# Projecting q and k of fourteen batches with seven quarter products instead of eight, on one Trainium2 core

## The chip, the cores and the metric

The kernel runs on one core of one Trainium2 chip. The metric is the device time of one launch in microseconds (us). All arithmetic is fp32.

## The reference, cut to what matters

`x` is 16 batches of 256 tokens by 512 features. First comes an attention layer with a residual, then a GRU over the 256 steps with a residual.

```
xn  = rms_norm(x) * g_norm * (1 + scale) + shift      # scale, shift from cond @ W_emb + b_emb
qkv = xn @ W_qkv                                      # 512 x 1536: q, k, v, 16 heads of 32
q, k = rms_norm(q) * g_q, rms_norm(k) * g_k           # per head of 32
o   = softmax(q k^T / sqrt(32)) v ;  x = x + o + o @ W_out
x   = x + GRU(x, W_ih, W_hh, b_ih, b_hh, h0 = cond)   # 256 steps, 16 batches side by side
```

The change is in one product of this: the 256 x 512 `xn` of a batch with the 512 x 1024 columns of `W_qkv` that give q and k.

## The kernel before, in words

The program has a short start (projection of `cond`, batch 0), then the attention of the 16 batches, then the GRU. The order of TensorE, VectorE, ScalarE and GpSimd is written out by hand: each engine runs its instructions in the order in which the code records them, and an instruction that waits holds up all that stand behind it on its engine. SyncE's DMA issues are ordered by a scheduler.

Attention is a pipeline over slots. Batch `b` has four slots, one for each group `g` of four heads. In slot `g` of batch `b` TensorE first makes the logits of the group (`logits_by_key`, L606, into the four PSUM banks `lg0` to `lg3`). ScalarE takes their exponentials (`exps_by_key`, L620) and GpSimd adds the two halves of each (`sums`, L622). The group of the slot before is multiplied with v (`weigh_by_key`, L634 and L644) and VectorE divides it (`put_weighed_by_key`, L658 to L663: transpose, reciprocal, transpose, multiply). Between these stand the steps for batch `m = b+1`: its q and k are projected (`project_qk`, L281, four calls of 64 matrix instructions), squared on ScalarE (L294), summed by head on VectorE (L298), turned to a factor (`Rsqrt`: L183, then Ln and Exp on ScalarE, L185 and L186, then three small VectorE operations, L190 to L193), multiplied by it (`norm_qk`, L309), transposed (`turn_qk`, L324), and q is scaled on GpSimd (`scale_q`, L334); v is projected (`project`, L262) and copied out by ScalarE (`put_v`, L303). Steps for batch `b+2` turn its tokens (`turn_x`, L236, `put_x`, L252 and L254), and steps for batch `b+3` take its token norms (`norm_first`, L209) and apply them (`norm_apply`, L220).

Every matrix product of this stage is cut into four column groups of 32 outputs that run side by side (the index `j`), and each fp32 product takes two matrix instructions. A call of `project_qk` makes 64 tokens by 1024 columns, with 256 moving columns in an instruction:

```
for k in ks:
    for i in range(2):
        t = n * P + 64 * m + 32 * i
        for j in range(HG):
            nc.tensor.matmul(a[32 * j : 32 * j + 32, i * T : (i + 1) * T],
                             batches[b].xnT[:, k, t : t + 32], w[:, k, j], ...)
```

The remaining four PSUM banks, `A`, `X`, `Y` and `Z`, hold the projections, the turned tokens and the weighed groups in turn. `w_a` is one 24 KB region in a partition: `W_emb` at the start, the normed tokens `xs` and the `squares` during attention, and `W_ih` for the GRU; `w_b` (`wq`) holds `W_qkv` and later `W_hh`.

Of the kernel before, what the change touches and what calls it, by code (L numbers as in the profile page):

```python
# [8 lines left out]
F32 = mybir.dt.float32  # L9
AF = mybir.ActivationFunctionType  # L10
ALU = mybir.AluOpType
# [9 lines left out]
def kernel(  # L21
# [69 lines left out]
    def load_tokens(xt, b):  # L91
        nc.sync.dma_start(xt, x[b].rearrange("(n p) d -> p n d", p=P))
# [26 lines left out]
    def program(ctx, bounded):  # L119
# [4 lines left out]
        small = work.enter_context(tc.tile_pool(name="small", bufs=4))  # L124
        ps_lg = ctx.enter_context(tc.tile_pool(name="ps_lg", bufs=1, space=PSUM))
        ps = ctx.enter_context(tc.tile_pool(name="ps", bufs=1, space=PSUM))
        x_tiles = dict(enumerate(x_first))

        def load_x(b):
            xt = p2.tile([P, NT, D], F32, tag="x", name=f"x_{b}")  # L130
            load_tokens(xt, b)
            x_tiles[b] = xt

        xs = w_a[:, KC * 2 * D : KC * 2 * D + NT * D].rearrange("p (n d) -> p n d", n=NT)
        squares = w_a[:, KC * 2 * D + NT * D : KC * 3 * D].rearrange("p (i n) -> p i n", i=2)
        wih = w_a.rearrange("p (k n) -> p k n", k=KC)

        b_more = p1.tile([P, 2, P], F32, name="b_more")

# [28 lines left out]
        def tile_ps(name, bank, shape=(P, D)):  # L168
            pool = ps if len(bank) == 1 else ps_lg
            return pool.tile(list(shape), F32, tag=bank, name=name)  # L170
# [31 lines left out]
        def norm_first(b, parts=range(NT)):  # L202
            if parts[0] == 0:
                batches[b].ssx = small.tile([P, NT], F32, tag="ssx", name=f"ssx_{b}")
                batches[b].rs = Rsqrt(batches[b].ssx, D, NT, f"x{b}")
            for n in parts:

                unused = xs[:, n, :] if b != 2 else spare(f"squares_{n}")
                nc.scalar.activation(  # L209
                    unused, x_tiles[b][:, n, :], AF.Square,  # L210
                    accum_out=batches[b].ssx[:, n : n + 1],
                )

# [4 lines left out]
        def norm_apply(b, rstd):  # L218
            for n in range(NT):
                nc.vector.tensor_scalar(  # L220
                    xs[:, n, :], x_tiles[b][:, n, :], rstd[:, n : n + 1],
                    None, ALU.mult,
                )
            batches[b].xnT = p1.tile([P, KC, T], F32, tag="xnT", name=f"xnT_{b}", bufs=2)
            if 0 < b and b + 2 < B:
                load_x(b + 2)

# [8 lines left out]
                nc.tensor.transpose(dst[r], src[q], ident[q, q])  # L236

        def turn_x(b, banks):
            tps = [tile_ps(f"tpx_{b}_{r}", banks[r], (P, KC, NT, QR)) for r in range(R)]
            for c in range(KC):  # L240
                for n in range(NT):
                    turn_block(
                        [tp[:, c, n, :] for tp in tps], xs[:, n, c * P : (c + 1) * P]
                    )
            return tps
# [25 lines left out]
        def project_qk(b, n, m, ks, a):  # L271
# [17 lines left out]
                        )  # L289
            return a  # L290

        def square(b, n, s, a):
            sq = spare(f"sq_{b}_{n}_{s}") if b == 0 else squares[:, s]
            nc.scalar.activation(sq, a, AF.Square)  # L294
            return sq
# [4 lines left out]
        def put_v(b, n, a):  # L300
            if n == 0:
                batches[b].v = p2.tile([P, NT, D], F32, tag="v", name=f"v_{b}")
            nc.scalar.copy(batches[b].v[:, n, :], a)  # L303

        def norm_qk(b, n, accs, rstd):
            out = []
            for s in range(2):
                qk = p1.tile([P, H, DH], F32, tag="qkn", name=f"qkn_{b}_{n}_{s}", bufs=2)
                nc.vector.tensor_tensor(  # L309
                    qk,  # L310
                    accs[s].rearrange("p (h d) -> p h d", d=DH),
                    rstd[:, s * H : (s + 1) * H].unsqueeze(2).to_broadcast([P, H, DH]),
                    ALU.mult,
                )
                out.append(qk.rearrange("p h d -> p (h d)"))
            return out
# [345 lines left out]
            nc.vector.transpose(rden, inv.to_broadcast([P, T // DH, DH]))  # L662
            nc.vector.tensor_tensor(oT[:, w.g, :, w.b], w.o[:, 0, :], rden, ALU.mult)  # L663

        def fast_slot0(b, w, prev, st):
            m = b + 1
            if b == 0:
                project(b, 1, 2, (3,), st.v1)
            put_v(b, 1, st.v1)
            exps_by_key(w)  # L670
            if b == 0:
                put_x(1, 0, st.tpx)
                put_x(1, 1, st.tpx, engine=nc.scalar)
                batches[2].rs.first()
                norm_apply(2, batches[2].rs.second())
            weigh_by_key(prev, "Y")
            st.q = project_qk(m, 0, 0, range(KC), "A")
            put_weighed_by_key(prev)
            tpx = turn_x(b + 2, "ZY") if b + 2 < B else None
            st.s0 = Stats(m, 0)  # L680
            sq = st.s0.square(0, st.q)
            if tpx:
                put_x(b + 2, 0, tpx)
                put_x(b + 2, 1, tpx, engine=nc.scalar)
            st.k = project_qk(m, 0, 1, (0, 1, 2), "X")
            st.s0.add(0, sq)

        def fast_slot1(b, w, prev, st):
            m = b + 1
            exps_by_key(w)  # L690
            project_qk(m, 0, 1, (3,), st.k)
            weigh_by_key(prev, "Y")
            put_weighed_by_key(prev)
            sq = st.s0.square(1, st.k)
            st.q1 = project_qk(m, 1, 0, range(KC), "Z")
            st.s0.add(1, sq)
            st.s0.rs.first()
            if b + 3 < B:
                norm_first(b + 3, (0,))
            st.s1 = Stats(m, 1)  # L700
            st.rstd = st.s0.rs.second()
            st.sq = st.s1.square(0, st.q1)

        def fast_slot2(b, w, prev, st):
            m = b + 1
            exps_by_key(w)
            qk0 = norm_qk(m, 0, (st.q, st.k), st.rstd)
            k = project_qk(m, 1, 1, (0, 1), "Y")
            weigh_by_key(prev, "X")
            project_qk(m, 1, 1, (2, 3), k)  # L710
            turn_qk(m, 0, qk0)
            scale_q(m, 0)
            put_weighed_by_key(prev)
            sq = st.s1.square(1, k)
            st.s1.add(0, st.sq)
            st.v0 = project(m, 0, 2, (0, 1), "A")
            st.s1.add(1, sq)
            st.s1.rs.first()
            if b + 3 < B:
                norm_first(b + 3, (1,))  # L720
                batches[b + 3].rs.first()
            if b == 0:
                for c in range(KC):
                    d = wo[:, c, c * P : (c + 1) * P]
                    nc.vector.tensor_tensor(d, d, ident, ALU.add)
                load_small()
            elif b == 2:
                for i in range(2):
                    a = b_rows[:, 2 * i, :]
                    nc.vector.tensor_tensor(a, a, b_more[:, i, :], ALU.add)  # L730
            st.accs = (st.q1, k)

        def fast_slot3(b, w, prev, st):
            m = b + 1
            exps_by_key(w)
            if b == 4:
                load_rows(wih, w_ih, (0, 1))
            elif b == 6:
                for i in range(4):
                    load_block(i)  # L740
            elif b == B - 3:
                load_rows(wih, w_ih, (2,))
            elif m == B - 1:
                load_rows(whh, w_hh, cols=slice(0, 2 * D))
                load_rows(wih, w_ih, (3,))
            qk1 = norm_qk(m, 1, st.accs, st.s1.rs.second())
            project(m, 0, 2, (2, 3), st.v0)
            st.v1 = project(m, 1, 2, (0, 1), "X")
            weigh_by_key(prev, "Z")
            project(m, 1, 2, (2, 3), st.v1)  # L750
            turn_qk(m, 1, qk1)
            scale_q(m, 1)
            put_v(m, 0, st.v0)
            put_weighed_by_key(prev)
            if b + 3 < B:
                norm_apply(b + 3, batches[b + 3].rs.second())
            if m == B - 1:
                put_v(m, 1, st.v1)

        TI = 16  # L760
        first = []
# [163 lines left out]
        with tc.manual_schedule(engines=ORDERED):  # L925
# [48 lines left out]
            for ks, n in (((0,), 0), ((0,), 1), ((1,), 0), ((1,), 1), ((2, 3), 0), ((2, 3), 1)):  # L974
                for i in range(2):
                    accs[n][i] = project_qk(0, n, i, ks, accs[n][i])
            v = project(0, 0, 2, range(KC), "lg0")
            s0, s1 = Stats(0, 0), Stats(0, 1)
            norm_first(1)
            batches[1].rs.first()  # L980
# [23 lines left out]
            for b in range(B - 1):  # L1004
                for g in range(NG):
                    if bounded:
                        w = logits_by_key(b, g)
                        (fast_slot0, fast_slot1, fast_slot2, fast_slot3)[g](b, w, prev, st)
                    else:
                        w = logits(b, g)  # L1010
                        (slot0, slot1, slot2, slot3)[g](b, w, prev, st)
                    prev = w
# [233 lines left out]
```

## Time and profile before

| | |
|---|---|
| median of 3 runs | 1658.77 us (1658.73 to 1660.42) |
| the profiled execution: its own time, its span | 1657.48 us, 1655.7 us |
| busy: TensorE, VectorE, ScalarE, GpSimd | 1638.1, 909.5, 536.7, 271.3 us |
| attention, slots of batches 0 to 14 | 34.4 to 508.2 us |
| one batch of it, from the same slot to the same slot | 31.5 us |
| busy in such a batch: VectorE, ScalarE, GpSimd | 18.2, 15.7, 12.6 us |
| granted TensorE clock | 0.999 |

The profile shows one execution, its times counted from the start of the span. 1.8 us of the execution's own time lie outside the span, and the execution was 1.3 us faster than the median of the runs. In a row of the timeline stand start, length, engine, source line and operation, the tiles written and read with their shapes, and the number of instructions merged in the row; in brackets stands the idle time before it and what ended it. The length of a row of matrix instructions runs to the modelled end of its last one, and the next row begins before that: rates are read from start to start. `PE` is TensorE, `DVE` VectorE, `ACT` ScalarE, `POOL` GpSimd.

### The profile page before, as it was taken

How to read it: one execution, taken by the hardware profiler on the slowest of the kernel's cores; microseconds unless marked ns; L12 is line 12 of the kernel's file. 1: busy time of each engine (PE TensorE's matmuls, PEld its weight loads, DVE VectorE, ACT ScalarE, POOL GpSimd, SP SyncE). 2: the span in 40 equal slices, each digit the busy share in tenths (PEclk: the TensorE clock that was granted, in tenths of full speed). 3: DMA queues.
4: the chain of work that ended last, by engine and by line, in shares of the span. 5: the costliest groups of instructions: out<-in, count | busy, mean ns of one | idle time of the engine just before them, and what ended most of it. 6: DMA issues, size and time to landing. Idle time of an engine off the chain costs nothing.

```text
span 1655.7 us, 93929 instructions
## 1 busy us (share of the span) xinstructions
PE 1638.1 (99%) x42901; PEld 1254.2 (76%) x42901; DVE 909.5 (55%) x3060; ACT 536.7 (32%) x1728; POOL 271.3 (16%) x534
## 2 busy tenths in 40 slices
PE   8999999999999999999999999999999999999997
PEld 4554554554555888888888888888888888888886
DVE  4566565556555555555555555555555555555554
ACT  4455444454443222222222222222222222222222
POOL 0334343343341000000000000000000000000000
PEclk9999999999999999999999999999999999999999
DMA  5300000000004000100000000000000010000000
GB/s 215 92 15 16 26 15 15 28 15 15 14 14 105 25 17 17 23 23 17 17 17 22 22 20 17 17 19 22 23 17 17 17 24 17 11 11 11 14 14 18
DMA packets 51178, 44.35 MB, mean 27 GB/s; under 512 B 10407, under 2 KB 43475, under 8 KB 50771
## 3 DMA queue, kind: packets, MB, share of 16 engines
q1 hardware_dynamic: 50663, 38.20, 8.6%
q8 instruction: 337, 5.52, 1.4%
q14 instruction: 70, 0.57, 0.1%
q10 hardware_dynamic: 108, 0.06, 0.0%
HBM read 29.79 MB, written 8.39 MB: 23 GB/s over the span
## 4 chain that ended last, share of the span: by engine, by line
PE 96%; DVE 2%; ACT 1%; issue 1%; DMA 0%; ACTq 0%; DVEq 0%
PE gr L807 26%; PE gz L807 19%; PE gn L807 14%; PE qk L281 14%; PE qkv L262 7%; PE o L1035 6%; PE lg L606 4%; PE o L634 3%; PE o L644 2%; PE tpx L236 1%; PE first L768 0%; DVE trh L1084 0%; ACT n L1163 0%; DVE n L1161 0%; DVE n L1162 0%
## 5 line engine op out<-in xcount | busy, mean ns | idle before, releaser
L807 PE MATMUL gr<-w_a,xT 128*32 128x256 f32 x4096 | 267.7, 379 | 0.0
L281 PE MATMUL qk<-w_b,xnT 128*32 128x256 f32 x4096 | 238.6, 380 | 1.2 <-DVE xnT L254 1.2
L1157 ACT ACTIVATE r<-trr 128x64 f32<-128x64 f32 x256 | 65.5, 256 | 514.8 <-DVE trr L1084 512.8
L1084 DVE STREAM_TRANSPOSE trr<-gr 128x128 f32<-128x128 f32 x256 | 81.1, 317 | 274.8 <-PE gr L807 274.8
L622 POOL TENSOR_TENSOR sums<-e 128x256 f32<-128x256 f32 x240 | 168.3, 733 | 310.0 <-ACT e L620 310.0
L281 PEld LDWEIGHTS qk<-w_b,xnT 128*32 128x32 f32 x4096 | 128.8, 110 | 92.5 <-issue 9.5
L807 PEld LDWEIGHTS gr<-w_a,xT 128*32 128x32 f32 x4096 | 133.1, 110 | 84.6
L1163 ACT ACTIVATE n<-n 128x64 f32<-128x64 f32 x256 | 65.6, 256 | 308.1 <-DVE n L1162 305.2
L620 ACT ACTIVATE e<-lg 128x512 f32<-128x512 f32 x256 | 131.9, 602 | 54.1 <-PE lg L606 54.0
L1035 PE MATMUL o<-oT,wo 128*32 128x256 f32 x1920 | 147.3, 379 | 0.0
L1084 DVE STREAM_TRANSPOSE trh<-gn 128x128 f32<-128x128 f32 x256 | 81.0, 317 | 116.9 <-PE gn L807 116.9
L807 PE MATMUL gr<-w_b,padded 128*32 128x128 f32 x4096 | 135.7, 273 | 2.7 <-DVE padded L1191 1.4
L807 PEld LDWEIGHTS gr<-w_b,padded 128*32 128x32 f32 x4096 | 114.7, 110 | 30.5 <-DVE padded L1191 29.9
L807 PE MATMUL gz<-w_b,padded 128*32 128x128 f32 x4096 | 135.3, 273 | 0.0
L807 PE MATMUL gn<-w_b,padded 128*32 128x128 f32 x4096 | 135.3, 273 | 0.0
L807 PE MATMUL gz<-w_a,xT 128*32 128x128 f32 x4096 | 135.3, 273 | 0.0
L807 PE MATMUL gr<-w_b,h 128*16 128x128 f32 x4064 | 134.3, 273 | 0.4
L807 PE MATMUL gz<-w_b,h 128*16 128x128 f32 x4064 | 134.2, 273 | 0.0
L807 PE MATMUL gn<-w_b,h 128*16 128x128 f32 x4064 | 134.2, 273 | 0.0
L807 PEld LDWEIGHTS gz<-w_a,xT 128*32 128x32 f32 x4096 | 117.2, 110 | 21.9
L1193 POOL TENSOR_TENSOR y<-xT,padded 128x64 f32<-128x64 f32 x128 | 41.0, 320 | 534.9 <-DVE padded L1191 534.9
L1193 POOL TENSOR_TENSOR y<-xT,h 128x64 f32<-128x64 f32 x127 | 40.7, 321 | 499.1 <-DVE h L1191 499.1
(125 smaller groups left out, 2233.4 us busy)
## 6 DMA issues: line engine op xcount, KB each, us to landing
xin<-in_x_dram SPq DMA_DIRECT2D x256, 32.0 KB, 2.5
out_dram<-osb SPq DMA_DIRECT2D x248, 32.0 KB, 2.5
x<-in_x_dram SPq DMA_DIRECT2D x14, 512.0 KB, 3.4
w_b<-in_L_cond_W_qkv_dram SPq DMA_DIRECT2D x4, 768.0 KB
w_a<-in_L_cond_W_ih_dram SPq DMA_DIRECT2D x16, 192.0 KB, 4.8
w_a<-in_L_cond_W_emb_dram SPq DMA_DIRECT2D x4, 512.0 KB, 3.5
w_b<-in_L_cond_W_hh_dram SPq DMA_DIRECT2D x16, 128.0 KB, 3.2
oT<-in_x_dram SPq DMA_DIRECT2D x2, 512.0 KB
```

The lines of the kernel that those rows point to most:

```text
L262: nc.tensor.matmul(a[32 * j : 32 * j + 32, :], batches[b].xnT[:, k, n * P + 32 * j : n * P + 32 * j + 32], wq[:, k, s * D : (s + 1) * D], ...
L281: nc.tensor.matmul(a[32 * j : 32 * j + 32, i * T : (i + 1) * T], batches[b].xnT[:, k, t : t + 32], w[:, k, j],  start=(k == 0 and i == 0), ...
L606: nc.tensor.matmul(w.lg[i][:, k, :], batches[b].qkT[r, NG + g, k * P : (k + 1) * P], batches[b].qkT[r, g, :], start=True, stop=True,)
L620: nc.scalar.activation(w.e[i], w.lg[i], AF.Exp)
L622: nc.gpsimd.tensor_tensor(w.sums[:, i, :], w.e[i][:, 0, :], w.e[i][:, 1, :], ALU.add)
L634: nc.tensor.matmul(w.o[i * DH : (i + 1) * DH, 0, :], v[:, k, h * DH : (h + 1) * DH], w.e[i][:, k, :], start=(k == 0), stop=(k == NT - 1),)
L807: nc.tensor.matmul(dst[32 * j : 32 * j + rows], stationary, w[:, k, :].rearrange("p (g j c) -> p j g c", g=3, c=P)[:, j, first::2][:, : ds ...
L1035: nc.tensor.matmul(acc[32 * j : 32 * j + 32, :], w[:, k, P * j + 32 * m : P * j + 32 * m + 32], rhs, start=(k == 0), stop=(k == KC - 1),)
L1084: nc.vector.transpose(tr.rearrange("p q s b -> p (q s b)"), gate)
L1157: nc.scalar.activation(r, turned("r", t, gr[:, 0, :])[:, :, s, :], AF.Sigmoid)
L1163: nc.scalar.activation(n, n, AF.Tanh)
L1193: (nc.gpsimd if t + 1 < T else nc.vector).tensor_tensor(y[:, :, tl * B : (tl + 1) * B], xTs[grp][:, :, ti, :], h, ALU.add)
```

## The change

The product of a batch is cut in two along the tokens (`n`), the contraction (`i`) and the columns (`h`: heads 0 to 7 and 8 to 15 of both q and k). Eight quarter products of 128 x 256 by 256 x 512 would give the four results. The change makes them from seven, by Strassen's scheme in the form with three sums of weights plus one made in place (`T3`, `T2`, `T4`, and `W01 - W00` in the place of `W01`), made once, and four sums of x (`S1` to `S4`) for each batch. All these sums run on GpSimd.

- Batches 0 and 1 are projected as before. From batch 2 on (`b >= 1`), the slots are `quarter_slot0` to `quarter_slot3`; the old functions serve `b = 0` alone as `first_slot0` to `first_slot3`.
- `multiply` makes one quarter product: 64 matrix instructions of 128 moving columns.
- The products stay in PSUM and are added up there where they can be: `z` in bank `A` takes four products in turn, `q7` in bank `Y` two, `q2` in bank `X` one. Three states of `z` are copied to SBUF by ScalarE (`keep`), and VectorE adds them to the others (`add_kept`).
- `norm_quarters` norms and transposes two results at a time and has GpSimd scale their q half. Three of the four results are normed from SBUF and not from PSUM.
- The order of the slots is new. A batch begins in slot 3 of the batch before (`begin_quarters`). Projection of v stands in slots 1, 2, 3 and the next slot 0. The turned tokens go to `lg2` and `lg3` and not to `Z` and `Y`.
- Weight sums lie in the first half of `w_a`, x sums in the next sixth. So `W_ih` is loaded only in slot 3 of batch 14, with the first four blocks of GRU input and two thirds of `W_hh`. Token tiles come from the pool of the GRU's input blocks, by two DMAs a batch and not one.

```diff
...
+        def add_weights(dst, a, op, b):
+            for k in range(2):
+                nc.gpsimd.tensor_tensor(dst[:, k], a[:, k], b[:, k], op)
+        def make_w_sums():
+            add_weights(w_sum(T3), w_half(1, 1), ALU.subtract, w_half(0, 1))
+            add_weights(w_sum(T2), w_sum(T3), ALU.add, w_half(0, 0))
+            add_weights(w_sum(T4), w_half(1, 0), ALU.subtract, w_sum(T2))
+        def make_last_w_sum():
+            add_weights(w_half(0, 1), w_half(0, 1), ALU.subtract, w_half(0, 0))
...
+        def make_x_sum(b, i):
+            a, op, c = {
+                S1: (x_part(b, 1, 0), ALU.add, x_part(b, 1, 1)),
+                S2: (x_sums[:, S1], ALU.subtract, x_part(b, 0, 0)),
+                S3: (x_part(b, 0, 0), ALU.subtract, x_part(b, 1, 0)),
+                S4: (x_part(b, 0, 1), ALU.subtract, x_sums[:, S2]),
+            }[i]
+            nc.gpsimd.tensor_tensor(x_sums[:, i], a, c, op)
+        def multiply(a, stationary, w, name=None):
+            start = isinstance(a, str)
+            if start:
+                a = tile_ps(name, a)
+            w = w.rearrange("p k s (g j d) -> p k j s g d", j=HG, d=DH)
+            for k in range(2):
+                for i in range(4):
+                    for j in range(HG):
+                        nc.tensor.matmul(
+                            a[32 * j : 32 * j + 32, i * P : (i + 1) * P],
+                            stationary[:, k, 32 * i : 32 * i + 32],
+                            w[:, k, j],
+                            start=(start and k == 0 and i == 0),
+                            stop=(k == 1),
+                            skip_group_check=True,
+                        )
+            return a
...
+        def norm_quarters(b, which, accs, rstd, fresh):
+            for s in range(2):
+                n, h = which[s]
+                a = dst = accs[s].rearrange("p (h d) -> p h d", d=DH)
+                if fresh[s]:
+                    dst = p1.tile([P, D], F32, tag="qkn", name=f"c_{b}_{n}_{h}", bufs=3)
+                    dst = dst.rearrange("p (h d) -> p h d", d=DH)
+                nc.vector.tensor_tensor(
+                    dst, a,
+                    rstd[:, s * H : (s + 1) * H].unsqueeze(2).to_broadcast([P, H, DH]),
+                    ALU.mult,
+                )
+                t = slice(n * P, (n + 1) * P)
+                nc.vector.transpose(
+                    batches[b].qkT.rearrange("p (s h g) t -> p s h g t", s=2, h=2)[
+                        :, :, h, :, t
+                    ].rearrange("p s g (i t) -> p i s g t", i=4),
+                    dst.rearrange("p h d -> p (h d)"),
+                )
+                q = batches[b].qkT[:, 2 * h : 2 * h + 2, t]
+                nc.gpsimd.tensor_scalar(q, q, g_col, 1.0, ALU.mult, ALU.mult)
...
+        def begin_quarters(m, st):
+            st.z = multiply("A", x_part(m, 0, 0), w_half(0, 0), f"z_{m}")
+            st.q7 = multiply("Y", x_sums[:, S3], w_sum(T3), f"q7_{m}")
+            st.z1 = keep(m, 1, st.z)
+        def quarter_slot0(b, w, prev, st):
+            m = b + 1
+            if b == 1:
+                put_v(b, 1, st.v1)
+            exps_by_key(w)
+            weigh_by_key(prev, "X")
+            if b > 1:
+                project(b, 1, 2, (2, 3), st.v1)
+                put_v(b, 1, st.v1)
+            tpx = turn_x(b + 2, ("lg2", "lg3")) if b + 2 < B else None
+            put_weighed_by_key(prev)
+            if tpx:
+                put_x(b + 2, 0, tpx)
+                put_x(b + 2, 1, tpx, engine=nc.scalar)
+            a = multiply("X", x_part(m, 0, 1), w_half(1, 0), f"q2_{m}")
+            st.c11 = add_kept(m, 0, 0, a, st.z1)
+            multiply(st.z, x_sums[:, S2], w_sum(T2))
+            st.z2 = keep(m, 2, st.z)
+        def quarter_slot1(b, w, prev, st):
+            m = b + 1
+            exps_by_key(w)
+            multiply(st.z, x_sums[:, S1], w_half(0, 1))
+            weigh_by_key(prev, "X")
+            z4 = keep(m, 4, st.z)
+            st.sa, st.sb = Stats(m, 0), Stats(m, 1)
+            sq = st.sa.square(0, st.c11)
+            st.c22 = add_kept(m, 1, 1, st.q7, z4)
+            st.sa.add(0, sq)
+            put_weighed_by_key(prev)
+            multiply(st.z, x_sums[:, S4], w_half(1, 1))
+            sq = st.sa.square(1, st.c22)
+            st.v0 = project(m, 0, 2, (0,), "Z")
+            if m + 1 < B:
+                make_x_sum(m + 1, S3)
+            st.sa.add(1, sq)
+            st.sa.rs.first()
+            sq = st.sb.square(0, st.z)
+            st.ra = st.sa.rs.second()
+            st.sb.add(0, sq)
+            if b + 3 < B:
+                norm_first(b + 3, (0,))
+        def quarter_slot2(b, w, prev, st):
+            m = b + 1
+            batches[m].qkT = p1.tile([P, 2 * NG, T], F32, tag="qkT", name=f"qkT_{m}", bufs=2)
+            exps_by_key(w)
+            norm_quarters(m, ((0, 0), (1, 1)), (st.c11, st.c22), st.ra, (False, False))
+            weigh_by_key(prev, "X")
+            multiply(st.q7, x_part(m, 1, 1), w_sum(T4))
+            put_weighed_by_key(prev)
+            if b + 3 < B:
+                norm_first(b + 3, (1,))
+                batches[b + 3].rs.first()
+            st.c21 = add_kept(m, 1, 0, st.q7, st.z2)
+            sq = st.sb.square(1, st.c21)
+            project(m, 0, 2, (1, 2, 3), st.v0)
+            if m + 1 < B:
+                make_x_sum(m + 1, S1)
+                make_x_sum(m + 1, S2)
+            st.sb.add(1, sq)
+            st.sb.rs.first()
+            put_v(m, 0, st.v0)
+            st.rb = st.sb.rs.second()
+            if b == 2:
+                for i in range(2):
+                    a = b_rows[:, 2 * i, :]
+                    nc.vector.tensor_tensor(a, a, b_more[:, i, :], ALU.add)
+        def quarter_slot3(b, w, prev, st):
+            m = b + 1
+            exps_by_key(w)
+            norm_quarters(m, ((0, 1), (1, 0)), (st.z, st.c21), st.rb, (True, False))
+            weigh_by_key(prev, "X")
+            st.v1 = project(m, 1, 2, (0, 1), "Z")
+            put_weighed_by_key(prev)
             if b + 3 < B:
                 norm_apply(b + 3, batches[b + 3].rs.second())
             if m == B - 1:
+                for i in range(4):
+                    load_block(i)
+                load_rows(whh, w_hh, cols=slice(0, 2 * D))
+                load_rows(wih, w_ih)
+                project(m, 1, 2, (2, 3), st.v1)
                 put_v(m, 1, st.v1)
+            else:
+                make_x_sum(m + 1, S4)
+                begin_quarters(m + 1, st)
...
             v = project(0, 0, 2, range(KC), "lg0")
+            if bounded:
+                make_w_sums()
             s0, s1 = Stats(0, 0), Stats(0, 1)
```

In `first_slot3` the end is new: `make_last_w_sum()`, the four x sums of batch 2 and `begin_quarters(2, st)`.

## Prediction

> **What bounds the kernel now.** I read the page first: busy times, then the chain that ended last.
>
> ```profile
> PE 1638.1 (99%) x42901; PEld 1254.2 (76%) x42901; DVE 909.5 (55%) x3060; ACT 536.7 (32%) x1728; POOL 271.3 (16%) x534
> PE 96%; DVE 2%; ACT 1%; issue 1%; DMA 0%; ACTq 0%; DVEq 0%
> ```
>
> TensorE is never idle for long, and 96% of the chain is its own work: whatever leaves TensorE is a gain, unless another engine then makes it wait. Next the timeline of TensorE, for the rate of the old instructions and of one that looks like the new ones (the rows from 900 are in the GRU).
>
> ```profile
> 259.39 3.64 PE L281 MATMUL qk<-w_b,xnT 128*32 128x256 f32 x64
> 262.96 0.71 PE L236 MATMUL tpx<-ident,w_a 64*128 64x64 f32 x16
> ...
> 900.04 1.06 PE L807 MATMUL gz<-w_a,xT 128*32 128x128 f32 x32
> 900.91 1.06 PE L807 MATMUL gr<-w_b,h 128*16 128x128 f32 x32
> ```
>
> 64 instructions of 256 columns take 3.57 us from start to start, 3.45 without the change of form at the end (the chain lists this call with 3.45 in each batch): 53.9 ns each. 32 instructions of 128 columns take 0.87 us, 27.2 ns each, though each loads its own weights.
>
> Then all engines around slot 1 of a batch, since the new results pass through ScalarE and VectorE in order.
>
> ```profile
> 267.40 1.07 PE L281 MATMUL qk<-w_b,xnT 128*32 128x256 f32 x16
> 267.55 2.07 ACT L620 ACTIVATE e<-lg 128x512 f32<-128x512 f32 x4 [2.30 <-PE lg L606]
> 269.47 0.63 ACT L294 ACTIVATE w_a<-qk 128x512 f32<-128x512 f32 x1
> 269.91 0.45 DVE L658 STREAM_TRANSPOSE den<-o 128x256 f32<-128x256 f32 x1 [4.25 <-PE o L644]
> 271.56 0.66 DVE L298 TENSOR_REDUCE ssqk<-w_a 128x16 f32<-128x512 f32 x1
> 272.26 0.32 ACT L185 ACTIVATE y_qk<-ssqk,eps 128x32 f32<-128x32 f32 x1 [2.15 <-DVE ssqk L298]
> 272.61 0.23 ACT L186 ACTIVATE y_qk<-y_qk 128x32 f32<-128x32 f32 x1
> 272.75 0.61 ACT L209 ACTIVATE w_a<-x 128x512 f32<-128x512 f32 x1
> 272.87 0.19 DVE L190 SCALAR_TENSOR_TENSOR u_qk<-y_qk 128x32 f32<-128x32 f32 x1 [0.43 <-ACT y_qk L186]
> 273.36 0.58 ACT L294 ACTIVATE w_a<-qk 128x512 f32<-128x512 f32 x1
> ```
>
> Read the steps from start to start: exponentials 0.15 us after the logits, the next ScalarE step 1.92 later; one `put_weighed_by_key` holds VectorE 1.65; from the end of the head sums to Exp's end 0.62; a token norm holds ScalarE 0.61.
>
> Last, what GpSimd does to VectorE, where both happened to meet.
>
> ```profile
> 62.27 0.18 DVE L190 SCALAR_TENSOR_TENSOR u_qk<-y_qk 128x32 f32<-128x32 f32 x1
> 62.47 2.11 POOL L622 TENSOR_TENSOR sums<-e 128x256 f32<-128x256 f32 x3 [4.40 <-ACT e L620]
> 62.49 0.77 DVE L191 TENSOR_TENSOR u_qk<-u_qk,m_qk 128x32 f32<-128x32 f32 x1
> 63.29 0.66 DVE L193 SCALAR_TENSOR_TENSOR y_qk<-u_qk,y_qk 128x32 f32<-128x32 f32 x1
> 63.98 0.69 DVE L309 TENSOR_TENSOR qkn<-qk,y_qk 128x512 f32<-128x512 f32 x1
> ```
>
> The small operations of L191 and L193 (both inputs in SBUF) need 0.19 us, but 0.77 and 0.66 under GpSimd's sums: each waits for the GpSimd operation under way (0.70 apart). L309, with one input in PSUM, keeps its 0.69.
>
> **TensorE's gain.** A batch loses 4 x 3.45 = 13.8 us and gets 7 x 64 x 27.2 ns = 12.2: 1.53 less with unrounded rates, 21.4 for 14 batches. Logits, weighing, v and turned tokens stay, with as many changes of form. The Trainium skill, "TensorE: Matmul & The Clock Gate", Back-to-back issue gap, speaks against this: it gives a sustained 81 ns for 128 columns and 131 for 512. My estimate from it, by a straight line, is 98 ns for 256, so that seven products of 128 would cost 1.44 times the old eight, some 6 us more a batch. The rows say 1.01 for the same columns in twice the instructions, and I take the rows.
>
> **The new wait.** In slot 3 `project(m, 1, 2, (0, 1))` writes bank `Z`, which `put_v(m, 0)` must have emptied. `put_v` stands on ScalarE behind Ln and Exp of `sb`, and these end a chain that begins in slot 1. Time 0 is the first matrix instruction of slot 1 after its logits.
>
> TensorE gets there so: S1 1.75, weighing 1.29 (0.86 + 0.43), S4 1.75, a quarter of v 0.87, logits 1.18, weighing 1.32, T4 1.75, v 2.60, logits 1.18, weighing 1.32: 15.0.
>
> The chain: exponentials 0.15; `keep` of z4 at 2.07, done 2.67 (a copy, L303, is 0.60); `c22` 2.70; VectorE's next, the head sums of `c11`, 0.61 later at 3.31; 0.65 for these; `put_weighed` 3.96 to 5.61; head sums of `c22` to 6.28; Ln and Exp 6.31 to 6.89; then on ScalarE the square of `z` at 6.80, the token norm 7.29, and only at 7.90 the exponentials of slot 2. VectorE: factor 6.92 to 7.60, head sums of `z` 7.52, first product of `norm_quarters` 8.17 to 8.85, transpose 8.88, second product 9.49, transpose 10.20, `put_weighed` 10.80, `m_x` 12.45, `c21` 12.53 to 13.22 (both as L309, 0.685). Square 13.25 to 13.86, head sums to 14.56, Ln and Exp from 14.60, `put_v` 15.09 to 15.69. TensorE goes on at 15.74, 0.74 late.
>
> That is with a clean port. GpSimd's sums of slot 2 start at 8.64 (0.74 after the exponentials), are held by the first product to about 8.8 and then run back to back, followed by two q scalings and sums S1 and S2, to 14 or so. The second product has both inputs in SBUF and falls at 9.49, as GpSimd's second sum begins: 0 to 0.70. L191's row is nearest, and I take the whole 0.70: stall 1.44. `m_x`, one input, at 12.45, has no row under a busy GpSimd: 0 to 0.6; L309, though larger, did not wait, so I take 0. `c11`, `c22`, `c21`, head sums and transposes have at most one SBUF input or are like rows that did not wait.
>
> Other waits I find covered, with their margins: `weigh` into `X` in slot 3 (0.9 us after `put_weighed`), z2 and z4 kept before the next product into `A` (0.3), `q2` into `X` (0.4), logits of the next batch after GpSimd's scaling (0.4). If the last cover is gone, GpSimd's queue behind late exponentials sets the pace; each 0.1 costs 1.4 in all.
>
> **Start.** `make_w_sums` gives GpSimd six operations of 512 columns. From 0.733 us at 256 columns and 0.320 at 64 (L1193), 1.28 each: 7.7. They need the third and fourth chunk of W_qkv, used without a stop by TensorE at 19.9 and 21.6, so they run from some moment in 15 to 20 until 23 to 28. VectorE's three small operations of batch 1's token factor stand at 22.80 to 23.35 and wait up to 1.28 each: 0 to 4 with the two operations of `norm_apply` behind them; I take 2.3. The chain from there ends in the first logits, and TensorE already waits for it:
>
> ```profile
> 34.39 1.15 PE L606 MATMUL lg<-qkT 32*128 32x256 f32 x16 [0.60 <-ACT qkT L332]
> ```
>
> **End and transfers.** In batch 14 no `begin_quarters` stands ahead of the last batch's logits, so these wait for GpSimd's scaling: `put_v` end + 4.9 (0.6 to the sums, 2.8 for them, 0.7 for VectorE's hold, 0.8 for two half-size scalings of L334) against + 3.6 on TensorE: 1.3. The late weight loads are 80 issues of about 0.5 us (L165: 16 in 8.16), 41 us in all. The four blocks go early, `W_hh` can start once S4 is done in slot 1 of batch 14, and 46 issues of W_ih and W_hh from there end about 26 us later, some 8 before the recurrent products need them: nothing. Were that cover gone, at most as much again. `last_w_sum` and the first x sums (8.9 us after slot 3 began, first use at 9.4) are just hidden. x loads in two DMAs: nothing, SyncE waits most of the time.
>
> **Sum.** 1657.48 - 21.4 + 14 x 1.44 + 2.3 + 1.3 = 1659.8 for the profiled execution. The median stood 1.3 above it: 1661.
>
> **The rivals.** *Clean port:* the second product slips between two GpSimd operations, as VectorE does without loss elsewhere; for it, it falls on the boundary; against it, GpSimd asks first. Stall 0.74, 9.8 less: 1651. *Slower, the port twice:* in slot 2 the shared port holds VectorE a second time on the chain (at `m_x`, or the first product if the chain is 0.5 later), another 0.6: stall 2.0, 1669. It decides from a stall of 1.51 on, that is when the chain loses 0.77 to the port. The Trainium skill, "SBUF — State Buffer", Who interferes with whom, supports this one: one-input `tensor_scalar` may use both ports too and is then fully blocked; no row here shows it. By it the sum would be 1669, by L309's row 1661. *No wait in slot 3:* ScalarE and VectorE are 0.8 faster than read; the gain stays whole, 1641. All rows speak against it.
>
> **How the numbers follow.** Forecast 0.37, clean port 0.30, port twice 0.27, no wait 0.06. A measurement of this kernel tells 0.2% (3.3 us) from no change. Clean port and no wait are faster: 0.36. The forecast, 1656 to 1666 with start and end at their bounds, splits: 0.20 within, 0.17 slower; with the twice-held port slower is 0.44. Range: the clean port with a start at nothing, 1650, to the twice-held port with the start at 4 and a little more, 1672; outside lie the case without a wait and about as much above.
>
> **What would show it.** Right: TensorE idle in front of L267 once a batch, released by ScalarE's copy to `v`, about 1.4 us; products at 27.2 ns an instruction; the second L369 of slot 2 over 1.2 us long, the first 0.7; batches of 31.4 us. Wrong: batches near 30 us, idle time in front of logits released by GpSimd, or products above 28 ns.

## The result and the profile after

The changed kernel takes 1664.56 us (median of 7 executions, 1662.87 to 1666.18) against 1658.77 before (1657.35 to 1660.42): the ratio is 1.0034, with a 95% interval of 1.0022 to 1.0045. It is slower by 0.34%, more than the 0.2% that a measurement tells from no change. The profiled execution took 1663.97, of which the span is 1662.1.

First the page: the engines' busy time, and the chain of work that ended last, by engines.

```profile
PE 1620.9 (98%) x45589; PEld 1310.1 (79%) x45589; DVE 966.0 (58%) x3102; ACT 558.8 (34%) x1770; POOL 342.4 (21%) x626
PE 66%; DVE 2%; issue 0%; ACT 0%; DVEq 0%; POOL 0%; ACTq 0%
```

TensorE is busy 17.2 us less, yet the end comes later. The chain can't say why: followed back from the end it reaches only to 514.25 us, GpSimd's scaling of q ahead of the last logits, so its 66% (96% before) hold none of the batches. What happens there is read from the waits of TensorE (us in total, times, longest).

```profile
PE qkv L267 <- ACT v L395: 19.4, 14, 1.7
PE lg L699 <- ACT qkT L425: 2.5, 1, 2.5
...
PE lg L699 <- POOL qkT L382: 1.1, 1, 1.1
...
PE q L342 <- DVE oT L756: 0.8, 2, 0.5
PE q L342 <- POOL w_a L332: 0.6, 1, 0.6
PE tpx L240 <- ACT e L713: 0.5, 2, 0.3
```

The first line is the wait for `put_v(m, 0)`, once in each of the 14 batches; the second is the late start. A batch takes 31.49 us, as it did before: the wait takes back what the products gain. The timeline of slots 2 and 3 of one batch shows where the wait comes from.

```profile
249.67 0.68 DVE L369 TENSOR_TENSOR c<-c,y_qk 128x512 f32<-128x512 f32 x1
250.14 3.33 POOL L715 TENSOR_TENSOR sums<-e 128x256 f32<-128x256 f32 x4 [4.11 <-ACT e L713]
251.02 1.17 DVE L369 TENSOR_TENSOR c<-c,y_qk 128x512 f32<-128x512 f32 x1
...
254.35 0.73 POOL L332 TENSOR_TENSOR w_a<-xnT 128x256 f32<-128x256 f32 x1
254.46 0.64 DVE L188 TENSOR_SCALAR m_x<-ssx 128x2 f32<-128x2 f32 x1
255.01 0.68 DVE L359 TENSOR_TENSOR c<-q,kept 128x512 f32<-128x512 f32 x1
...
256.23 0.61 PE L737 MATMUL o<-sums,ones 128*32 128x256 f32 x8
...
257.60 0.57 ACT L395 COPY v<-qkv 128x512 f32<-128x512 f32 x1
...
258.22 1.92 PE L267 MATMUL qkv<-w_b,xnT 128*32 128x512 f32 x16 [1.38 <-ACT v L395]
...
259.96 1.93 PE L342 MATMUL z<-w_b,xnT 128*32 128x128 f32 x64
261.70 1.93 PE L342 MATMUL q<-w_a 128*32 128x128 f32 x64
```

The two products of `norm_quarters` in slot 2 (L369) have the same form, but the first takes 0.68 us and the second, under GpSimd's sums of the exponentials, 1.17. `m_x`, an operation on two columns, takes 0.64 under GpSimd's sum of x (0.15 elsewhere in the same trace). Then `c21` (L359) with one input in PSUM takes its 0.68 under the next sum of x. TensorE could have gone on at 256.66 (the eight weighings of 256.23 need 0.43 from start to start) and goes on at 258.22: a gap of 1.56. The bracket says 1.38, since it counts from a modelled end. The last two batches have no `m_x`; there the first product is held too (1.14 at 470.44), and the bracket is 1.29 and 1.28. The products run 1.74 us from start to start, 27.2 ns an instruction.

At the start the weight sums on GpSimd hold batch 1's three small operations.

```profile
20.38 2.52 POOL L312 TENSOR_TENSOR w_a<-w_a,w_b 128x512 f32<-128x512 f32 x2
21.75 1.18 DVE L188 TENSOR_SCALAR m_x<-ssx 128x2 f32<-128x2 f32 x1 [8.03 <-ACT w_a L214]
22.87 2.51 POOL L312 TENSOR_TENSOR w_a<-w_b,w_a 128x512 f32<-128x512 f32 x2
23.03 1.13 DVE L196 TENSOR_TENSOR u_x<-u_x,m_x 128x2 f32<-128x2 f32 x1
24.19 1.20 DVE L198 SCALAR_TENSOR_TENSOR y_x<-u_x,y_x 128x2 f32<-128x2 f32 x1
...
36.41 1.15 PE L699 MATMUL lg<-qkT 32*128 32x256 f32 x16 [2.46 <-ACT qkT L425]
37.49 1.67 PE L267 MATMUL qkv<-w_b,xnT 128*32 128x512 f32 x8
```

The first logits come at 36.41 instead of 34.39. The eight projections after the gap take 1.67 instead of 1.07: the granted clock was 0.78 from 35 to 40 us and 0.88 from 40 to 45 (1.00 before). In windows of 0.2 us it is 0.50 from 37.8 to 41.2 and 1.00 on either side. By slot 3 of batch 0 TensorE stands at 62.94 instead of 60.38.

### The profile page after: what moved, and what is told of

Its sections match the earlier page's. It is cut to its first block, busy times and chain, and to the rows that moved or that the text cites. A ratio compares the mean times of both kernels' runs of the same rounds, so it can differ in the third digit from the quotient of the medians.

```text
span 1662.1 us, 99577 instructions
## 1 busy us (share of the span) xinstructions
PE 1620.9 (98%) x45589; PEld 1310.1 (79%) x45589; DVE 966.0 (58%) x3102; ACT 558.8 (34%) x1770; POOL 342.4 (21%) x626
## 4 chain that ended last, share of the span: by engine, by line
PE 66%; DVE 2%; issue 0%; ACT 0%; DVEq 0%; POOL 0%; ACTq 0%
PE gr L975 26%; PE gz L975 19%; PE gn L975 14%; PE o L1209 6%; PE first L936 0%; DVE trh L1258 0%; PE lg L699 0%; ACT n L1337 0%; PE o L727 0%; DVE n L1335 0%; DVE n L1336 0%; PE o L737 0%; DVE padded L1364 0%; DVE padded L1363 0%; DVE padded L1365 0%
## 5 line engine op out<-in xcount | busy, mean ns | idle before, releaser
L975 PE MATMUL gr<-w_a,xT 128*32 128x256 f32 x4096 | 267.7, 379 | 0.0
L715 POOL TENSOR_TENSOR sums<-e 128x256 f32<-128x256 f32 x240 | 183.0, 793 | 235.0 <-ACT e L713 235.0
L267 PE MATMUL qkv<-w_b,xnT 128*32 128x512 f32 x1024 | 122.1, 596 | 19.4 <-ACT v L395 19.4
L975 PEld LDWEIGHTS gz<-w_b,padded 128*32 128x32 f32 x4096 | 114.5, 110 | 0.0
```

Source lines behind the costliest of these rows:

```text
L267: nc.tensor.matmul(a[32 * j : 32 * j + 32, :], batches[b].xnT[:, k, n * P + 32 * j : n * P + 32 * j + 32], wq[:, k, s * D : (s + 1) * D], ...
L715: nc.gpsimd.tensor_tensor(w.sums[:, i, :], w.e[i][:, 0, :], w.e[i][:, 1, :], ALU.add)
L975: nc.tensor.matmul(dst[32 * j : 32 * j + rows], stationary, w[:, k, :].rearrange("p (g j c) -> p j g c", g=3, c=P)[:, j, first::2][:, : ds ...
```

## The experiments

All are compared with 1664.56 for the changed kernel; the kernel before stood at 1657.2 to 1659.6 beside them. The theory: TensorE's gain is whole, and VectorE's operations on the chain through `sb` (the norm factors of the second pair of results), which GpSimd holds up, take it back ahead of `put_v`. The rival: TensorE itself sets the pace, and the products or the changes of form are dearer than read. `norm_quarters` is called in two slots, with two products each: "the second product" below is that of slot 2. An edit shifts the lines behind it: L271 of e2 is L267, L702 of e9 and L703 of e10 are L699.

**e1: v copied ahead of the square of `c21`.** This takes the end of the chain off `put_v`.

```diff
 st.c21 = add_kept(m, 1, 0, st.q7, st.z2)
-sq = st.sb.square(1, st.c21)
 project(m, 0, 2, (1, 2, 3), st.v0)
+put_v(m, 0, st.v0)
+sq = st.sb.square(1, st.c21)
 ...
-put_v(m, 0, st.v0)
```

> The copy of v out of bank Z (put_v of the first half) is recorded ahead of the square of c21, so that ScalarE makes it when the v projection ends and not after Ln and Exp. Theory (the 1.56 us that TensorE loses in each of 14 slots 3 are the wait for this copy): the wait goes, TensorE comes to the next batch's logits 1.56 earlier, and there GpSimd's scaling of q, which now ends 0.4 earlier, makes it wait 0.5 to 0.6: 1.0 a batch, 14 us in all, about 1650.5. Rival (another engine sets the pace of the batch, the copy is only the last to be seen): within 3 us of the changed kernel's 1664.6. A gain of the whole 22 us (1643) would say that the scaling is earlier than I read it.

Measured: 1655.88, ratio to before 0.9982 [0.9973, 0.9991]. The wait for `v` is gone, but a new one stands 2.5 us later in the same slot (first its line of the waits, then the timeline):

```profile
PE z L342 <- DVE c L369: 9.3, 13, 2.0
```
```profile
256.94 0.69 DVE L369 TENSOR_TENSOR c<-z,y_qk 128x512 f32<-128x512 f32 x1
...
257.68 1.96 PE L342 MATMUL z<-w_b,xnT 128*32 128x128 f32 x64 [0.60 <-DVE c L369]
```

`begin_quarters` writes bank `A`, which the same chain reads in the first product of slot 3. A batch takes 30.71 us instead of 31.49. So the chain was the cause, and taking its end off one reader let it reach the next: the gain was 8.7, not 14.

**e2: `m_x` moved behind the weighing of slot 3.** (`mean()` is the split-off first operation of `first()`.)

```diff
-    batches[b + 3].rs.first()                  # slot 2
+    batches[b + 3].rs.first(mean=False)
 ...
+    batches[b + 3].rs.mean()                   # slot 3
     norm_apply(b + 3, batches[b + 3].rs.second())
```

> m_x, the small VectorE operation on two columns that waits for GpSimd in slot 2 (0.64 us where it needs 0.17), is moved behind the put_weighed of slot 3, off the chain; ScalarE's Ln and Exp stay. Theory (the port holds the chain at m_x): c21 and all behind it come 0.47 earlier, the wait in slot 3 falls from 1.56 to 1.1, 6.6 us in all, about 1658. Rival (c21 waits for something else at that time): 1664.6 within 2 us.

Measured: 1659.57, ratio 1.0000 [0.9991, 1.0009]. The wait for `v` falls from 19.4 to 12.7 us in all, and only where there is an `m_x`: from 1.38 to 0.82 in a steady batch.

```profile
257.19 1.92 PE L271 MATMUL qkv<-w_b,xnT 128*32 128x512 f32 x16 [0.82 <-ACT v L399]
```

These 0.56 are the 0.55 by which `c21` started behind `m_x` in the changed kernel (254.46 to 255.01): 0.49 by which `m_x` was too long (0.64 against 0.15), the rest its own place. The last two batches, without `m_x`, stay at 1.27. A two-column operation cost this kernel 5.0 us.

**e3: the weight sums made in slot 1 of batch 0**, behind its exponentials, instead of at the start.

```diff
-            if bounded:
-                make_w_sums()                  # before batch 0
 ...
+            make_w_sums()                      # slot 1 of batch 0, after the exponentials
```

> make_w_sums is recorded behind the exponentials of slot 1 of batch 0 and not in the start. Theory (its six GpSimd operations hold VectorE's small operations of batch 1's token factor by 2 us on the way to the first logits): the first logits come at 34.4 again and not at 36.4, and 2 to 2.6 us go, about 1662.3. Rival (the late first logits have another reason, such as x arriving in two transfers): 1664.6. A small loss can come back if the three small operations held in slot 1 delay batch 1.

Measured: 1668.33, ratio 1.0060 [1.0047, 1.0074], a miss. The first logits do come early (21.0 us after the first projection, 23.3 in the changed kernel), but the sums hold the next chain:

```profile
55.57 1.32 DVE L195 SCALAR_TENSOR_TENSOR u_qk<-y_qk 128x32 f32<-128x32 f32 x1
55.58 2.50 POOL L312 TENSOR_TENSOR w_a<-w_a,w_b 128x512 f32<-128x512 f32 x2
...
60.82 1.93 PE L727 MATMUL o<-e,v 128*32 128x256 f32 x16 [2.50 <-DVE qkn L402]
```

0.19 us became 1.32 and the two operations after it 1.21 and 1.19; TensorE waited 2.50 and got a clock of 0.62 from 60 to 63 us and 0.81 from 63 to 66 (in windows of 0.2 us: 0.50 from 60.7 to 64.1). The cost moved and grew.

**e4: the product with the fourth weight sum left out of slot 2.**

```diff
-            multiply(st.q7, x_part(m, 1, 1), w_sum(T4))
```

> The product with T4 is left out in each of 14 batches (64 matrix instructions, 1.75 us of TensorE in slot 2, ahead of the wait in slot 3; the third and fourth result lack it). Theory (from slot 1 to the copy in slot 3 the batch is paced by the chain through ScalarE and VectorE, not by TensorE): TensorE only waits longer, 1.56 + 1.75, and the time stays at 1664.6 within 3 us. Rival (TensorE still sets the pace): 14 x 1.75 = 24.5 us less, 1640.

Measured: 1674.64, ratio 1.0093 [1.0077, 1.0108], outside both forecasts. TensorE has 14 x 1.75 = 24.5 us less to do and the kernel is 10 slower. There are two kinds of batch. Six of the twelve between slot 3 of batch 1 and slot 3 of batch 13 take 31.5 to 31.8 us, as in the changed kernel: a new wait of 1.1 and a longer one for `v` take up the freed 1.75. That rules out the rival: TensorE's work was not what bounded the batch. The six others have the same two waits and take 33.2. The timeline of one batch of each kind (the second from 259.86), and the windows at the place in the second (span; TensorE, weight load, VectorE, ScalarE and GpSimd busy; granted clock; DMA):

```profile
231.83 1.92 PE L267 MATMUL qkv<-w_b,xnT 128*32 128x512 f32 x16 [1.96 <-ACT v L395]
233.57 1.93 PE L342 MATMUL z<-w_b,xnT 128*32 128x128 f32 x64
...
259.86 1.07 PE L727 MATMUL o<-e,v 128*32 128x256 f32 x16 [1.10 <-DVE oT L756]
260.72 0.64 PE L737 MATMUL o<-sums,ones 128*32 128x256 f32 x8
263.31 2.75 PE L267 MATMUL qkv<-w_b,xnT 128*32 128x512 f32 x16 [1.95 <-ACT v L395]
265.81 2.85 PE L342 MATMUL z<-w_b,xnT 128*32 128x128 f32 x64
```
```profile
264.00:265.00 1.00, 1.00 (x11) 0.17 (x7) 0.97 (x3) 1.00 (x3) 1.00 (x2) 0.64 0.00 0
265.00:266.00 1.00, 1.00 (x12) 0.36 (x8) 0.97 (x2) 0.22 (x1) 1.00 (x2) 0.50 0.00 0
```

In the second kind the clock falls to 0.50 after the two waits (from 264.3 to 267.7 in windows of 0.2 us; 0.64 is a mean over a window that holds the fall), and instructions that took 1.92 and 1.93 us take 2.75 and 2.85. In the first kind it stays at 1.00. So the freed time was lost in waiting, and six times 1.68 us of slower work behind the waits are the 10 us. Why the clock falls in one batch and not in the next, these runs don't show.

**e8: no sums on GpSimd for the exponentials of slot 2**; TensorE weighs the four exponentials of a key one by one.

```diff
-            exps_by_key(w)                     # slot 2
+            exps_by_key(w, sums=False)
 ...
-            weigh_by_key(prev, "X")            # slot 3
+            weigh_by_key(prev, "X", sums=False)
```

> The changed kernel without GpSimd's sums of the exponentials of slot 2; TensorE's weighing takes the four exponentials of a key unsummed, which costs it about 0.43 us more a batch, ahead of the wait in slot 3. Theory: the VectorE operations on the chain in slot 2 were long because GpSimd held them. The second L369 of slot 2 goes from 1.17 back to about 0.7 us, put_v comes 0.5 to 0.96 earlier, and TensorE's gap in front of L267 falls from 1.56 to 0.2 to 0.6 us; the time is 1651 to 1657. Rival: the operation is long for its own sake (its two inputs, or its place behind the transposes): it stays at 1.17, the gap shrinks only by the 0.43 that TensorE does more, and the time stays at 1664.6.

Measured: 1656.34, ratio 0.9985 [0.9976, 0.9994]. The second product is short again, `m_x` under the sum of x is still long:

```profile
247.24 0.65 DVE L369 TENSOR_TENSOR c<-c,y_qk 128x512 f32<-128x512 f32 x1
...
250.17 0.57 DVE L188 TENSOR_SCALAR m_x<-ssx 128x2 f32<-128x2 f32 x1
...
253.86 1.93 PE L267 MATMUL qkv<-w_b,xnT 128*32 128x512 f32 x16 [0.37 <-ACT v L395]
```

The gap before L267 is 0.55 (the weighing before it starts at 252.45 and needs 0.86), the wait 4.7 us in all instead of 19.4, and gone in the last two batches, which have neither hold. So the product was long because GpSimd was at work. With the 0.43 that TensorE does more put back and the 0.42 of `m_x` taken off, a batch with neither hold would have a gap of 0.55 + 0.43 - 0.42 = 0.56.

**e5: e1, and q7 ahead of z where the quarters of a batch begin**; in batch 0 the sums of x come ahead of the last weight sum.

```diff
 def begin_quarters(m, st):
-    st.z = multiply("A", x_part(m, 0, 0), w_half(0, 0), f"z_{m}")
     ...                                        # q7, unchanged
+    st.z = multiply("A", x_part(m, 0, 0), w_half(0, 0), f"z_{m}")
```

> The copy of v early, and now also q7 ahead of z where a batch's quarters begin, with the sums of x for S3, S1 and S2 ahead of the last weight sum in batch 0. Theory: the 0.78 us a batch by which z's first product waited for bank A goes, because q7's 1.75 us now stand in front of it; against the version with the early copy alone that is 14 x 0.78 = 11 us, and 0.8 for q7 in batch 0, so 1655.9 - 11.8 = 1644, if nothing else is late. A limit behind it: the logits of the next batch would arrive about 0.4 us a batch before GpSimd has scaled q, which gives 6 back: 1649 to 1650. Rival: z's wait has its cause elsewhere (VectorE's chain as a whole sets the pace), the time stays at 1655.9 and the wait only changes its place.

Measured: 1652.12, ratio 0.9965 [0.9951, 0.9979], above both 1644 and 1649 to 1650. The wait for bank `A` is gone but for 0.2 us, and the logits of the next batch wait instead:

```profile
PE lg L699 <- POOL qkT L382: 8.2, 14, 2.1
```

I read this as GpSimd's queue (its scaling of q stands behind its sums) and made **e6** against it: e5, the later `m_x` of e2, the six weight sums on VectorE, and slot 3's scaling of q on ScalarE.

```diff
-                nc.gpsimd.tensor_scalar(q, q, g_col, 1.0, ALU.mult, ALU.mult)
+                nc.scalar.activation(q, q, AF.Copy, scale=g_col)     # in slot 3
```

> The edits of three versions together: v copied early, q7 ahead of z with the last weight sum later, the mean term of the GRU's norm (m_x) behind the weighing in slot 3, the first weight sums on VectorE, and the q scaling of slot 3 on ScalarE in place of GpSimd. Theory: TensorE has no wait of its own in a steady batch, so the whole gain of the quarter products shows: 1658.8 - 21.4 + about 0.3 for the start + 1.2 for the first two batches + 0.5 for the end = 1639 to 1641. Rival: the ScalarE scaling delays ScalarE's own queue and the wait returns there, 0.4 to 0.6 us a batch: 1645 to 1649.

Measured: 1644.47 (1643.55 to 1648.28), ratio 0.9915 [0.9902, 0.9929], faster than both kernels, but not the 1639 to 1641 of the forecast. **e9** has, beside e5's edits, the scaling alone:

> The version with v copied early and q7 ahead of z, and of the edits that the combined version adds only one: in slot 3, ScalarE scales q instead of GpSimd. Theory: of the 7.65 us between the two versions it is this edit that counts, because the logits of the next batch waited 8.2 us in all for GpSimd's scaling (14 waits, the last of 2.1), and neither the place of m_x nor the first weight sums ends a wait of TensorE any more. So some 6 to 7 less than 1652.1: 1645 to 1646. Rival: m_x or the first weight sums carry a part; then this version stays 2 us or more above the combined one, at 1647 to 1650.

Measured: 1651.56, ratio 0.9945 [0.9932, 0.9959]. My theory fell: 0.6 us of the 7.65 that lie between e5 and e6. The medians are of different rounds, in which the kernel before moved by 2 us too; the batch itself is firmer, and it went from 30.41 us in e5 to 30.34. Its logits still wait nearly every batch, since ScalarE's scaling is late too (the wait's label names a sum of x, which the logits do not read; it ends at the same moment as the scaling, 289.08):

```profile
286.62 1.16 DVE L369 TENSOR_TENSOR c<-c,y_qk 128x512 f32<-128x512 f32 x1
...
288.57 0.51 ACT L383 ACTIVATE qkT<-qkT,g_col 128x256 f32<-128x256 f32 x1 [1.32 <-DVE qkT L375]
...
289.17 1.15 PE L702 MATMUL lg<-qkT 32*128 32x256 f32 x16 [0.27 <-POOL w_a L332]
```

That points at the chain itself being late, and not at the queue of who scales. **e10** is e5 with only the later `m_x` (e2's diff), and **e11** is e6 with the weight sums back on GpSimd.

> The version with v copied early and q7 ahead of z, and of the combined version's edits only the later m_x (behind the weighing of slot 3); GpSimd still scales q and still makes the weight sums. Theory, formed on the run with the scaling alone: the chain through c21 ends in the next batch's logits, whoever scales q, and the hold of m_x lengthens it by 0.47 us a batch. In the version without the edit the logits waited 8.2 us in all; 0.47 less for each of 13 batches removes nearly all of the steady part: 1646 to 1647. Rival: both edits are needed, since GpSimd's sums of the exponentials of slot 3 end just ahead of its scaling and hold it back: 1649 to 1652.

> The combined version with the six first weight sums back on GpSimd; v early, q7 first, m_x late and ScalarE's scaling stay. Theory: the weight sums count for little, as in the version with these alone on VectorE: 1644.5 to 1646.5. Rival: the 2.27 us by which the first logits come earlier count in full once no later wait takes them up: 1646.7.

Measured: e10 1645.69, ratio 0.9928 [0.9915, 0.9942]; e11 1644.78, ratio 0.9927 [0.9913, 0.9940]. One operation of two columns, put elsewhere, carries 6.4 of the 7.65, 0.51 a batch (30.41 to 29.90); the rest is within what these runs tell apart. In e10 GpSimd still scales q, and in time for most logits:

```profile
PE lg L703 <- POOL qkT L386: 3.1, 4, 2.1
```
```profile
253.71 0.93 POOL L386 TENSOR_SCALAR qkT<-qkT,g_col 128x256 f32<-128x256 f32 x2
254.76 1.15 PE L703 MATMUL lg<-qkT 32*128 32x256 f32 x16
...
255.41 0.15 DVE L188 TENSOR_SCALAR m_x<-ssx 128x2 f32<-128x2 f32 x1
```

`m_x` has its 0.15 there, and a batch takes 29.90 us (247.04 to 276.94), 1.59 less than before the change. With three moves in the order of issue the products' gain thus shows whole, 1.59 x 14 = 22 us, of which 16.4 are left between slot 3 of batch 0 and the first recurrent product (451.5 us against 468.0). The last logits of slot 3 take 2.10 of the rest; the waits of the first two batches and a few single ones were not taken apart.

**e7: the first weight sums on VectorE, alone.**

```diff
-            make_w_sums()
+            make_w_sums(nc.vector)
```

> The changed kernel with the six first weight sums on VectorE instead of GpSimd, in the stretch from 14 to 22 us in which VectorE has little to do; the rest as it is. Theory: the late start (2.56 us by slot 3 of batch 0) came from GpSimd holding VectorE's three small operations of batch 1's token factor. Six VectorE operations of about 0.65 us fit before them, so the first logits come at 34.4 instead of 36.4 and the time falls by 2 to 2.5: 1662. Rival: the start's loss is taken up by a later wait in any case: 1664.6, no change.

Measured: 1664.53, ratio 1.0040 [1.0027, 1.0054]: no change. In the profile the reason for the late start is confirmed and the gain is lost again at once:

```profile
35.15 1.15 PE L699 MATMUL lg<-qkT 32*128 32x256 f32 x16 [0.19 <-ACT qkT L425]
...
42.98 1.24 PE L240 MATMUL tpx<-ident,w_a 64*128 64x64 f32 x16 [2.23 <-DVE w_a L225]
44.14 4.10 PE L286 MATMUL qk<-w_b,xnT 128*32 128x256 f32 x48
```

From the first projection to the first logits it takes 21.0 us instead of 23.3 (21.4 before). Then TensorE reaches a wait of 2.23 for VectorE that had been 1.12 when it came late, and the 48 instructions behind it took 4.10 instead of 2.80 at a clock of 0.82 (0.50 from 43.4 to 46.8 in windows of 0.2 us). The first projection itself began 1.0 us later in this execution, after loads that took longer; that belongs to no edit. How much of the start is to be had on average stays open.

## Why the prediction was right, and where not

**The products: right.** 27.2 ns an instruction, 1.74 us a product, as read off the recurrent part. The rule of the Trainium skill's "TensorE: Matmul & The Clock Gate", Back-to-back issue gap, 81 ns for 128 columns, does not hold here. A batch without waits (e10) takes 29.90 us, 1.59 less than before. The prediction gives 1.53, but its own figures, 13.8 less 7 x 64 x 27.2 ns, give 1.61; the difference is about 1 us in 14 batches.

**The wait in slot 3: right in place and cause, 1.56 us for 1.44.** On the prediction's clock (0 is the first matrix instruction of slot 1 after its logits, at 241.65) TensorE was to arrive at 15.0 and did at 15.01; `put_v` was to start 0.70 after 15.09, and did at 15.95. Two terms in it were mis-sized. The second product's hold, taken at 0.70, was 0.49. `m_x`, taken at 0 because the L309 row had not waited, was held 0.49: the step that failed is that comparison. L309 reads an input in PSUM, `m_x` only SBUF; its likeness to the rows of L191 counted, not its size or its number of inputs. Here the Trainium skill's "SBUF — State Buffer", Who interferes with whom, was right and the row I took against it was of another kind: e2 shows it. The clean gap, 0.74 on record, comes out at 1.56 - 0.49 - 0.49 = 0.58, and e8 gives 0.56. That the total came so near is in part luck: 0.16 and 0.21 too much, 0.49 too little.

**The rivals.** The port did hold VectorE twice on the chain, as the slower rival said, and the gap passed the 1.51 from which that one was to decide: by its mechanism this rival is what ran, and the forecast was nearer in the number only. But its price of 2.0 and 1669 was too high: the holds were 0.49 and 0.49 instead of 0.70 and 0.6, and the clean gap was 0.58 instead of 0.74. The clean port (1651) did not happen. That there would be no wait at all (1641) needed what e10 does, three pieces of work in another order, and even that took 1645.69.

**Start: 2.56 for 2.3**, by the mechanism named, and again with luck: the first logits come 2.02 late, the half clock of 3.4 us that the prediction did not have costs about 1.7, and the wait for batch 2's tokens is 1.15 shorter (1.12 for 2.27). **End: 1.3 for 1.3**, GpSimd's scaling ahead of the last logits. The late weight loads cost nothing, as said: no wait of TensorE for them is among its waits.

**Put at nothing, and wrong:** the prediction held the first sums of x "just hidden", ready 8.9 us after slot 3 began and needed at 9.4. The first was ready after 10.0 (62.94 to 73.0), and q7 waited about 0.8 us for it. In the same passage from batch 0 to 1 turned tokens waited 0.7 for exponentials and q2 0.7 for `X`, 2.2 together. For these two the prediction had shown the covers for a steady batch alone; the first one has a different order.

**The sum.** 1657.48 - 21.4 + 14 x 1.56 + 2.56 + 1.3 + 2.2 = 1664.0, against 1663.97 measured. That it closes so well is chance: with e10's 1.59 in place of 1.53 some 0.8 us stay open. The forecast for this execution was 1659.8, 4.2 less: 2.2 of it is the passage and 1.7 the gap. The median stood only 0.6 above the execution and not 1.3, so it fell 3.6 above 1661.

## What to carry to other kernels

When work leaves the bounding engine, follow the longest chain of the other engines to every place where it meets that engine again: here the next reader stood 2.5 us, and then a slot, behind the first, and moving one reader only showed the next. VectorE's products and scalar operations with all inputs in SBUF waited for the GpSimd operation under way, with 2 columns as with 512, so place them by what GpSimd does at that moment, off the chain. Check the covers for the first and the last pass of a loop separately.

## What was unexpected of the hardware

After waits of about 2 us TensorE's granted clock often fell, and the work behind them ran slower. In windows of 0.2 us it went to 0.50, stayed there for 3.4 us and returned to 1.00: after 2.46 us at the start of the changed kernel, after waits of 1.10 and 1.95 us close together in e4, after 2.50 in e3 and 2.23 in e7. It is not fixed: in e4 the same two waits had this in six of twelve batches (1.68 us each) and nothing in the others. The wait of 2.2 to 2.3 us for batch 2's tokens was followed by 1.00 in the kernel before, in e8 and e11, and by 0.50 in the nine other runs that have it. A steady batch with one gap of 1.56 kept 1.00. A wait of TensorE can thus cost more than its length, as in e4, where less work made the kernel slower.
